# Two-layer graph convolution on one core: last groups of 12 and 7 tiles, an early head of layer 2, layer 2 without node loads, and a first index column

## Chip, core and metric

The kernel runs on one core of a Trainium2 chip. The metric is device time in microseconds of one execution; lower is better. Times of "before" are a median of 10 runs. The engines are PE (matmuls), DVE (vector), ACT (activations and copies), POOL (here: memsets, iotas and the issue of gathers) and SP (issue of plain loads and stores).

## What is computed

Two relational graph convolutions over 12500 nodes of 128 features and 200000 edges sorted by destination, with 10 relations, a residual and a layer norm:

```python
def _rgcn_layer(x, src, dst, edge_type, w_rel, root, bias):
    seg = dst * NUM_REL + edge_type
    sums = segment_sum(x[src], seg)                 # per node and relation
    cnt = segment_sum(ones, seg)
    mean = (sums / maximum(cnt, 1.0)[:, None]).reshape(N, NUM_REL, -1)
    return einsum('nrd,rdo->no', mean, w_rel) + x @ root + bias

edge_type = argmax(msg[:, 16:26], axis=1)
h = relu(_rgcn_layer(x, src, dst, edge_type, w_rel1, root1, b1))
out = layernorm(x + _rgcn_layer(h, src, dst, edge_type, w_rel2, root2, b2))
```

Everything is float32. The mean is over the edges of one node and one relation.

## The kernel before, in words

**Tiles and groups.** 128 edges make a tile; there are NT = 1563 tiles. Tiles go in groups: 95 groups of G = 16 (NS = 95), and then 43 tiles in smaller groups. Before, these are 8, 8, 8, 8, 4, 4 and 3 (L68 to L72). `layer` (L545) runs over the groups once for layer 1 with the table `x`, once for layer 2 with the table `hD`, the hidden nodes in HBM.

**One group.** `gather` (L464) has POOL issue one indirect DMA per tile: 128 rows of the table, chosen by a column of `idxE`, into the buffer `g`, which holds 16 tiles and is taken from a ring of three (`RING = 3`). `ones` (L475) has DVE build, for each tile, `oh`: 128 edges x 120 columns (10 relations x 12 nodes from the tile's first on), with the edge's weight 1/count where it belongs and zero elsewhere (L481), and `at`, which says at which of 160 node columns each of the tile's 12 nodes stands (L485). `sums` (L488) multiplies `g` by `oh` on PE into the PSUM tile `zp` (L495), one matmul per tile, and ACT copies `zp` to `zs` (L509). Groups of 16 wait once for all their gathers; the groups at the end wait for each tile. `project` (L514) multiplies `zs` by the ten relation weights (L521, 20 instructions for up to 8 tiles, 40 for more), ACT copies the result to `ms`, and `add` (L532) multiplies `ms` by `at` (L537) and adds 160 columns to the transposed sums `acc` on DVE (L543). `zp` has one buffer, `oh` two.

**Blocks of nodes.** `starts` cuts the nodes into 29 blocks: 23 of 512, five of 128 and a last of 84. `done_after(k)` says after which tile all edges of block k have been added, with a margin. `block_in` (L394) loads the block's nodes (`xb`; in layer 2 also `hb` from `hD`), transposes them on PE (L407) and copies them to `fT`. `block_rows` adds the bias on DVE (`a`, L416), sets that part of `acc` to zero for layer 2 (L418), and multiplies with the root weights (L421) and the identity (L422). `hidden` (L429) applies ReLU (L435) and stores to `hD`; `final` (L438) adds `xb` (L447), normalises (L450 to L457) and stores. Block 26 is done after the tile 1543, block 28 (the last 84 nodes) after the last tile.

**Set-up.** Edges are prepared in 13 chunks of 128 tiles: `sources` loads the indices as rows, casts them to float, transposes them on PE and casts them back into `idxE` (L165, L172); `types` and `count` find the relation and the count of each edge. Chunk 0 comes ahead of the layers; the others are steps (`todo`), spread over layer 1's groups. ACT fills `acc` with zeros in 25 pieces (L615).

**Order.** Engines run their own queues in order. A scheduler orders the instructions of each engine by program order and by when their inputs are expected, so instructions of one block are interleaved with those of neighbouring groups. Pools decide when a buffer is free: `ps_f` (two PSUM banks, shared by `pf` tiles of blocks and of edge preparation), `gpool` (three), `fin` (one each). SP's queue carries all plain loads and stores in order; a load into a buffer waits for that buffer.

Of the kernel before, what the change touches and what calls it, by code (L numbers as in the profile page):

```python
# [9 lines left out]
F32 = mybir.dt.float32  # L10
BF16 = mybir.dt.bfloat16
I32 = mybir.dt.int32
# [8 lines left out]
P = 128  # L21
# [22 lines left out]
def rgcn_resnorm_kernel(ctx: ExitStack, tc: tile.TileContext, x, src, dst, attr, w_rel1, root1, b1,  # L44
# [25 lines left out]
    while t < NT:  # L70
        groups.append((t, min(HT if NT - t > 3 * QB else QB, NT - t)))
        t += groups[-1][1]  # L72
# [15 lines left out]

    HALF = NT * P - E
    assert C == P and E % GT == 0 and 0 < HALF < P and NT % CT and 1 < groups[-1][1] < groups[-2][1]  # L90

# [26 lines left out]
    wE = keep.tile([P, NCH * CT], F32, name="wE")  # L118

# [54 lines left out]

    ahead = []
# [217 lines left out]

    def block_in(k, l):  # L394

        n0, n, subs = block(k)
        last = "e" if k == NBLK - 1 else ""
        b = len(subs) if last else 4
        xb = fin.tile([P, b, C], F32, name="xb" + last)
        rows_dma(xb, x, k, False)  # L400
        fb = xb
        if l:
            fb = fin.tile([P, b, C], F32, name="hb" + last)
            rows_dma(fb, hD, k, False)
        pt = ps_f.tile([P, YB], F32, name="pf")
        for t, h in subs:
            nc.tensor.transpose(pt[:, t * P:t * P + h], fb[:h, t, :], ident[:h, :h])  # L407
        fT = fin.tile([P, b * P], F32, name="fT" + last)
        nc.scalar.activation(fT[:, :n], pt[:, :n], AF.Copy)  # L409
        return xb, fT  # L410

    def block_rows(fT, k, l):

        n0, n, subs = block(k)
        a = fin.tile([P, YB], F32, name="a")
        nc.vector.tensor_scalar(a[:, :n], acc[:, n0:n0 + n], bsb[l], None, op0=ALU.add)  # L416
        if l == 0:
            nc.vector.memset(acc[:, n0:n0 + n], 0.0)  # L418
        pr = ps_f.tile([P, 4, C], F32, name="pf")
        for t, h in subs:  # L420
            nc.tensor.matmul(pr[:h, t, :], fT[:, t * P:t * P + h], rsb[l], start=True, stop=False)  # L421
            nc.tensor.matmul(pr[:h, t, :], a[:, t * P:t * P + h], ident, start=False, stop=True)  # L422
        return pr
# [5 lines left out]
    def hidden(k, ready):  # L429

        xb, fT = ready
        pr = block_rows(fT, k, 0)
        hb = fin.tile([P, 4, C], F32, name="hb")
        for p, s in spans(k):
            nc.scalar.activation(hb[:p, s], pr[:p, s], AF.Relu)  # L435
        rows_dma(hb, hD, k, True)

    def final(k, ready):  # L438

        xb, fT = ready  # L440
        pr = block_rows(fT, k, 1)
        v = fin.tile([P, 4, C], F32, name="v")
        mv = small.tile([P, 4, 2], F32, name="mv")
        rstd = small.tile([P, 4], F32, name="rstd")
        _, n, subs = block(k)
        for p, s in spans(k):
            nc.vector.tensor_tensor(v[:p, s], pr[:p, s], xb[:p, s], op=ALU.add)  # L447
        for t, h in subs:
            st = small.tile([P, nc.vector.BN_STATS_DIM], F32, name="st")
            nc.vector.bn_stats(st[:h], v[:h, t, :])  # L450
            nc.vector.bn_aggr(mv[:h, t, :], st[:h])
        for p, s in spans(k):
            nc.scalar.activation(rstd[:p, s], mv[:p, s, 1], AF.Sqrt, bias=eps[:p])  # L453
            nc.vector.reciprocal(rstd[:p, s], rstd[:p, s])
        o = fin.tile([P, 4, C], F32, name="o")
        for t, h in subs:
            nc.vector.tensor_scalar(o[:h, t, :], v[:h, t, :], mv[:h, t, 0:1], rstd[:h, t:t + 1],  # L457
                                    op0=ALU.subtract, op1=ALU.mult)
        rows_dma(o, out, k, True)
# [3 lines left out]

    def gather(table, t0, n):  # L464
        g = gpool.tile([P, G, C], F32, name="g")
        return g, [then("POOL", nc.gpsimd.indirect_dma_start(  # L466
            out=g[:, j, :], out_offset=None, in_=table, in_offset=bass.IndirectOffsetOnAxis(
                ap=idxE[:, t0 + j:t0 + j + 1], axis=0))) for j in range(n)]
# [6 lines left out]
    def ones(k):  # L475

        t0, n = groups[k]
        oh = dpool.tile([P, G, KW], F32, name="oh")
        for j in range(n):
            t = t0 + j  # L480
            then("DVE", nc.vector.tensor_scalar(oh[:, j, :], iotaP[:, :KW], keyE[:, t:t + 1], wE[:, t:t + 1],  # L481
                                                op0=ALU.is_equal, op1=ALU.mult))
        at = spool.tile([HR, 2, SW], F32, name="at")
        for h, _ in halves(n):
            nc.vector.tensor_scalar(at[:, h, :], iotaP[:HR], place[:, h, k:k + 1], None, op0=ALU.is_equal)  # L485
        return oh, at

    def sums(table, k, oh, at):  # L488

        t0, n = groups[k]  # L490
        end = k >= NS
        g, gathers = gather(table, t0, n)
        zp = ps_z.tile([P, G // QB, YB], F32, name="zp")
        for j in range(n) if end else reversed(range(n)):
            m = nc.tensor.matmul(zp[:, j // QB, j % QB * KW:(j % QB + 1) * KW], g[:, j, :], oh[:, j, :],  # L495
                                 start=True, stop=True)
            then("PE", m)
            if end:
                continue
            if j < n - 1:  # L500
                tc.keep_in_program_order(m)
                continue

            for d in gathers[:j]:
                tc.add_manual_dep(m.ins, d.ins.name, whole, reason="one wait per group")
        zs = zpool.tile([P, NREL, G, WN], F32, name="zs")
        for b in range(-(-n // QB)):
            m = min(QB, n - b * QB)
            then("ACT", nc.scalar.activation(  # L509
                zs[:, :, b * QB:b * QB + m, :],  # L510
                zp[:, b, :m * KW].rearrange("c (j r n) -> c r j n", r=NREL, n=WN), AF.Copy))
        return k, zs, at
# [32 lines left out]
    def layer(table, l, finish, steps, flag_too=False):  # L545
# [8 lines left out]
        def add_oldest():  # L554
# [3 lines left out]
            while done < NBLK and sum(groups[k]) >= done_after(done):  # L558
                finish(done, ready if done == NBLK - 1 else given or block_in(done, l))
# [3 lines left out]
        for k in range(NG):  # L563
            end = k >= NS
            if k and not given and done < NBLK - 1:
                given = block_in(done, l)
            if projected:
                add_oldest()
            if end:
# [4 lines left out]
                if not ready:  # L574
                    ready = block_in(NBLK - 1, l)
# [6 lines left out]
            held.append(sums(table, k, *(made or ones(k))))  # L582
            made = ones(k + 1) if end and k < NG - 1 else None
# [27 lines left out]
    zero = fin.tile([P, YB], F32, name="a")  # L611
    nc.vector.memset(zero, 0.0)
    for a in range(0, NPAD, YB):
        m = min(NPAD - a, YB)
        nc.scalar.activation(acc[:, a:a + m], zero[:, :m], AF.Copy)  # L615
# [3 lines left out]
    weights_in()  # L619
    todo = []  # L620
    for c in range(1, NCH):
        s = [as_steps(sources, c + 1)] if c + 1 < NCH else []
        todo.append((c * CT // G - 2, [8 + L // DB + 2], chain(*s, types(c), count(c))))
# [22 lines left out]

    gp = ctx.enter_context(tc.tile_pool(name="gp", bufs=2))
# [120 lines left out]
    with tc.If(flag > 0):  # L768
# [3 lines left out]
        for l, (table, finish) in enumerate(((x, hidden), (hD, final))):  # L772
            nc.vector.memset(acc, 0.0)
# [29 lines left out]
```

## Time and profile before

| what | value |
|---|---|
| median of 10 runs | 3946.68 us (3943.41 to 3948.06) |
| the profiled execution | 3947.26 us |
| its span in the profile | 3945.4 us |
| POOL busy | 2957.1 us, 75% |
| PE busy | 2350.4 us, 60% |
| DVE busy | 1513.5 us, 38% |
| ACT busy | 528.5 us, 13% |
| gathers of layer 1 / layer 2 | 1563 / 1563, mean 946 / 944 ns |
| `zp` matmuls (L495) | 6252 instructions, 1149.2 us |
| projection matmuls (L521) | 7880 instructions, 899.0 us |
| `oh` (L481) | 3126, mean 391 ns |

The profile is of one execution; its times are from the start of its span. A line of the page's list of groups gives the source line, engine and operation, output<-input, shape and count, then busy time and mean duration in ns, then the engine's idle time ahead of these and what ended most of it. A line of the timeline gives start, duration, engine, line, operation and, in brackets, the idle time before it and what ended that. "issue" is time in which an engine waited for nothing that the profile shows. A float32 matmul appears as two instructions, a transpose as one.

### The profile page before, as it was taken

How to read it: one execution, taken by the hardware profiler on the slowest of the kernel's cores; microseconds unless marked ns; L12 is line 12 of the kernel's file. 1: busy time of each engine (PE TensorE's matmuls, PEld its weight loads, DVE VectorE, ACT ScalarE, POOL GpSimd, SP SyncE). 2: the span in 40 equal slices, each digit the busy share in tenths (PEclk: the TensorE clock that was granted, in tenths of full speed). 3: DMA queues.
4: the chain of work that ended last, by engine and by line, in shares of the span. 5: the costliest groups of instructions: out<-in, count | busy, mean ns of one | idle time of the engine just before them, and what ended most of it. 6: DMA issues, size and time to landing. Idle time of an engine off the chain costs nothing.

```text
span 3945.4 us, 43799 instructions
## 1 busy us (share of the span) xinstructions
PE 2350.4 (60%) x16206; PEld 2258.4 (57%) x16206; DVE 1513.5 (38%) x4660; ACT 528.5 (13%) x1142; POOL 2957.1 (75%) x3142
## 2 busy tenths in 40 slices
PE   4666665665666666566745565565655565556557
PEld 3655555565566565565635555555555555555556
DVE  6434444343443434443423333333333333333333
ACT  2111111111111111111101111111111111111111
POOL 7777777777777777777677777777777777777775
PEclk8877777777777777777867777777777777777778
DMA  5322323223223232222222222222222222222222
GB/s 163 90 73 75 95 59 89 88 66 90 74 74 95 58 89 64 63 62 57 63 58 58 61 69 61 61 61 64 66 61 61 61 69 61 61 61 69 61 59 55
DMA packets 180538, 278.99 MB, mean 71 GB/s; under 512 B 55608, under 2 KB 127175, under 8 KB 177191
## 3 DMA queue, kind: packets, MB, share of 16 engines
q0 software_dynamic: 100032, 205.07, 19.8%
q1 hardware_dynamic: 78577, 71.03, 5.6%
q8 instruction: 132, 2.16, 0.2%
q14 instruction: 89, 0.73, 0.1%
q10 hardware_dynamic: 1708, 0.01, 0.0%
HBM read 262.28 MB, written 13.60 MB: 70 GB/s over the span
## 4 chain that ended last, share of the span: by engine, by line
POOL 68%; issue 26%; DMA 3%; PE 2%; ACT 0%; DVE 0%; POOLq 0%; ACTq 0%
POOL g L466 68%; DMA g<-hD,idxE 2%; DMA g<-in_x_dram,idxE 1%; PE pp L521 1%; PE zp L495 1%; PE pp L537 0%; ACT zs L509 0%; PE pf L422 0%; PE pf L421 0%; DVE acc L543 0%; POOLq L466 0%; ACT ms L527 0%; DVE o L457 0%; ACT rstd L453 0%; DVE st L450 0%
## 5 line engine op out<-in xcount | busy, mean ns | idle before, releaser
L495 PE MATMUL zp<-oh,g 128*128 128x120 f32 x6252 | 1149.2, 360 | 1517.4 <-DMA g<-hD,idxE 802.4
L495 PEld LDWEIGHTS zp<-oh,g 128*128 128x128 f32 x6252 | 1108.0, 274 | 1556.1 <-issue 1475.7
L466 POOL DMA_INDIRECT g<-hD,idxE x1563 | 1475.7, 944 | 488.4 <-issue 477.3
L466 POOL DMA_INDIRECT g<-in_x_dram,idxE x1563 | 1478.6, 946 | 476.9 <-issue 468.1
L481 DVE TENSOR_SCALAR oh<-bank,keyE,wE 128x120 f32<-128x120 f32 x3126 | 1002.5, 391 | 719.7 <-PE zp L495 719.5
L521 PE MATMUL pp<-w,zs 128*96 128x128 f32 x7880 | 899.0, 273 | 17.5 <-ACT zs L509 14.3
L521 PEld LDWEIGHTS pp<-w,zs 128*96 128x96 f32 x7880 | 871.1, 163 | 23.4 <-ACT zs L509 18.5
L509 ACT ACTIVATE zs<-zp 128x480 f32<-128x480 f32 (+1 forms) x782 | 386.0, 576 | 2508.7 <-PE zp L495 2508.4
L543 DVE TENSOR_TENSOR acc<-acc,pp 128x160 f32 x204 | 65.4, 321 | 1379.2 <-PE pp L537 1378.9
L537 PE MATMUL pp<-at,ms 96*128 96x160 f32 (+1 forms) x788 | 211.0, 407 | 6.9 <-ACT ms L527 5.1
L537 PEld LDWEIGHTS pp<-at,ms 96*128 96x128 f32 (+1 forms) x788 | 171.1, 271 | 22.9 <-ACT ms L527 15.9
L527 ACT ACTIVATE ms<-pp 96x256 f32<-96x256 f32 (+1 forms) x198 | 74.3, 375 | 451.1 <-PE pp L521 451.1
L485 DVE TENSOR_SCALAR at<-bank,place 96x160 f32<-96x160 f32 x394 | 132.7, 369 | 0.0
L362 DVE TENSOR_TENSOR eqb<-pf,kh 128x1344 bf16<-128x1344 f32 (+2 forms) x65 | 100.2, 1549 | 75.4 <-PE pf L366 67.7
L422 PE MATMUL pf<-ident,a 128*128 128x128 f32 x392 | 83.0, 296 | 2.0 <-DVE a L416 1.9
L421 PE MATMUL pf<-root,fT 128*128 128x128 f32 x388 | 80.1, 290 | 1.1 <-ACT fT L409 1.1
L422 PEld LDWEIGHTS pf<-ident,a 128*128 128x128 f32 x392 | 66.2, 212 | 3.5 <-DVE a L416 2.9
L421 PEld LDWEIGHTS pf<-root,fT 128*128 128x128 f32 x388 | 64.3, 208 | 2.0 <-ACT fT L409 2.0
L435 ACT ACTIVATE hb<-pf 128x512 f32<-128x512 f32 (+2 forms) x29 | 15.4, 530 | 340.8 <-PE pf L422 338.6
L364 PE MATMUL pf<-eqb,identb 128*128 128x512 bf16 (+2 forms) x130 | 50.3, 387 | 11.1 <-DVE eqb L362 11.1
L366 PE MATMUL pf<-eqb,identb 128*128 128x512 bf16 (+2 forms) x130 | 50.5, 389 | 0.0
L447 DVE TENSOR_TENSOR v<-pf,xb 128x512 f32<-128x512 f32 (+1 forms) x28 | 17.4, 620 | 73.7 <-PE pf L422 73.6
(107 smaller groups left out, 453.8 us busy)
## 6 DMA issues: line engine op xcount, KB each, us to landing
m<-in_edge_attr_dram SPq DMA_DIRECT2D x24, 1344.0 KB
g<-in_x_dram,idxE POOLq DMA_INDIRECT x1563
g<-hD,idxE POOLq DMA_INDIRECT x1563
xb<-in_x_dram SPq DMA_DIRECT2D x46, 256.0 KB
hD<-hb SPq DMA_DIRECT2D x23, 256.0 KB
hb<-hD SPq DMA_DIRECT2D x23, 256.0 KB
out_dram<-o SPq DMA_DIRECT2D x23, 256.0 KB
w<-in_L_gnn_w_rel_dram SPq DMA_DIRECT2D x2, 640.0 KB
```

What stands on the lines that cost most here:

```text
L362: nc.vector.tensor_tensor(eq[:p], kp[:p, None, :R].to_broadcast([p, DB, R]), fore, op=ALU.is_equal)
L421: nc.tensor.matmul(pr[:h, t, :], fT[:, t * P:t * P + h], rsb[l], start=True, stop=False)
L422: nc.tensor.matmul(pr[:h, t, :], a[:, t * P:t * P + h], ident, start=False, stop=True)
L466: return g, [then("POOL", nc.gpsimd.indirect_dma_start(out=g[:, j, :], out_offset=None, in_=table, in_offset=bass.IndirectOffsetOnAxis(ap= ...
L481: then("DVE", nc.vector.tensor_scalar(oh[:, j, :], iotaP[:, :KW], keyE[:, t:t + 1], wE[:, t:t + 1], op0=ALU.is_equal, op1=ALU.mult))
L485: nc.vector.tensor_scalar(at[:, h, :], iotaP[:HR], place[:, h, k:k + 1], None, op0=ALU.is_equal)
L495: m = nc.tensor.matmul(zp[:, j // QB, j % QB * KW:(j % QB + 1) * KW], g[:, j, :], oh[:, j, :], start=True, stop=True)
L509: then("ACT", nc.scalar.activation(zs[:, :, b * QB:b * QB + m, :], zp[:, b, :m * KW].rearrange("c (j r n) -> c r j n", r=NREL, n=WN), AF.C ...
L521: nc.tensor.matmul(po[:m * WN, h], zs[:, r, h * HT:h * HT + m].rearrange("c j n -> c (j n)"), wsb[l][:, r, :], start=(r == 0), stop=(r == ...
L527: nc.scalar.activation(ms[:, :n // HT], po[:HR, :n // HT], AF.Copy)
L537: nc.tensor.matmul(pa, ms[:m * WN, h], at[:m * WN, h], start=(h == 0), stop=(h == len(parts) - 1))
L543: nc.vector.tensor_tensor(acc[:, s], acc[:, s], pa, op=ALU.add)
```

## The change

1. The last 43 tiles make groups of 8, 8, 8, 12 and 7, five groups instead of seven. Two consecutive groups that fit into 16 tiles share one buffer `g`.
2. The first 16 tiles of layer 2 gather only from the first EARLY = 12288 nodes, with indices held below that (`idxH`) and weights set to zero for edges from later nodes (`wH`). Those edges' part comes from `late_h`, the last two blocks (128 + 84 = 212 nodes) kept in SBUF, by matmuls with `late_w`, tables built by `head()` during layer 1's last full groups.
3. Layer 2 loads no nodes. `hidden` now also transposes its result, multiplies it by layer 2's root weights, and writes that plus layer 2's bias plus the node itself into `acc` in place of the zeros. `final` transposes `acc` by a matmul with the identity and normalises from PSUM. Layer 1's bias is put into `acc` by the fill at the start, which therefore comes after the weights' loads in the program.
4. The indices of the first tile are also loaded directly as a column, `idx0`, and only the first gather of layer 1 uses it.
5. Chunk 12 of the edge preparation is to end four groups earlier, and `head()` is one more step behind it.

The part of the program behind `tc.If(flag > 0)` is a slow path for other inputs; it doesn't run here.

```diff
     while t < NT:
-        groups.append((t, min(HT if NT - t > 3 * QB else QB, NT - t)))
+        n = NT - t
+        groups.append((t, HT if n > 2 * HT + QB else HT + QB if n > HT + QB else n))
         t += groups[-1][1]
...
+    EARLY = starts[NBLK - 2]
...
+    idx0 = keep.tile([P, 1], I32, name="idx0")
+    nc.sync.dma_start(idx0, src[0:P].rearrange("(e o) -> e o", o=1))
     ahead = []
     first_index = sources(0)
...
     def block_in(k, l):
+        if l:
+            return None
...
-        if l:
-            fb = fin.tile([P, b, C], F32, name="hb" + last)
-            rows_dma(fb, hD, k, False)
...
-        a = fin.tile([P, YB], F32, name="a")
-        nc.vector.tensor_scalar(a[:, :n], acc[:, n0:n0 + n], bsb[l], None, op0=ALU.add)
-        if l == 0:
-            nc.vector.memset(acc[:, n0:n0 + n], 0.0)
...
+    def hidden(k, fT):
+        n0, n, subs = block(k)
+        pr = ps_f.tile([P, 4, C], F32, name="pf")
+        for t, h in subs:
+            nc.tensor.matmul(pr[:h, t, :], fT[:, t * P:t * P + h], rsb[0], start=True, stop=False)
+            nc.tensor.matmul(pr[:h, t, :], acc[:, n0 + t * P:n0 + t * P + h], ident, start=False, stop=True)
+        i = k - (NBLK - 2)
+        hb = late_h[:, i:i + 1] if i >= 0 and not anew else fin.tile([P, 4, C], F32, name="hb")
         for p, s in spans(k):
             nc.scalar.activation(hb[:p, s], pr[:p, s], AF.Relu)
         rows_dma(hb, hD, k, True)
+        pt = ps_f.tile([P, YB], F32, name="pf")
+        for t, h in subs:
+            nc.tensor.transpose(pt[:, t * P:t * P + h], hb[:h, t, :], ident[:h, :h])
+        hT = fin.tile([P, YB], F32, name="hT")
+        nc.scalar.activation(hT[:, :n], pt[:, :n], AF.Copy)
+        po = ps_f.tile([P, YB], F32, name="pf")
+        nc.tensor.matmul(po[:, :n], rsb[1], hT[:, :n], start=True, stop=True)
+        nc.vector.scalar_tensor_tensor(acc[:, n0:n0 + n], po[:, :n], bsb[1], fT[:, :n], op0=ALU.add, op1=ALU.add)
...
+    def final(k, _):
+        n0, n, subs = block(k)
+        v = ps_f.tile([P, 4, C], F32, name="pf")
...
-            nc.vector.tensor_tensor(v[:p, s], pr[:p, s], xb[:p, s], op=ALU.add)
+            nc.tensor.matmul(v[:h, t, :], acc[:, n0 + t * P:n0 + t * P + h], ident, start=True, stop=True)
...
+    def head():
+        nc.vector.tensor_scalar(idxH, idxE[:, :G], EARLY - 1, None, op0=ALU.min)
...
+        for b in range(0, G, QB):
+            pm = [ps_f.tile([P, YB], F32, name="pf") for _ in range(2)]
+            for j in range(QB):
+                t = b + j
+                oh = prep.tile([P, KW], F32, name="ohH")
+                nc.vector.tensor_scalar(oh, iotaP[:, :KW], keyE[:, t:t + 1], wE[:, t:t + 1],
+                                        op0=ALU.is_equal, op1=ALU.mult)
+                for i in range(2):
+                    of = prep.tile([P, P], F32, name=f"of{i}")
+                    nc.vector.tensor_scalar(of, iotaP[:, :P], off[:, i, t:t + 1], None, op0=ALU.is_equal)
+                    nc.tensor.matmul(pm[i][:, j * KW:(j + 1) * KW], of, oh, start=True, stop=True)
+            for i in range(2):
+                nc.scalar.activation(late_w[i][:, b * KW:(b + QB) * KW], pm[i][:, :QB * KW], AF.Copy)
+            yield
...
     def gather(table, t0, n):
-        g = gpool.tile([P, G, C], F32, name="g")
+        o = shared.get("to", G)
+        if o + n > G:
+            o = 0
+            shared["g"] = gpool.tile([P, G, C], F32, name="g")
+        shared["to"] = o + n
+        g = shared["g"][:, o:o + n]
+        ix = idxE
+        if is_head(table, t0):
+            table, ix = table[:EARLY, :], idxH
...
+                    nc.tensor.matmul(z[:, :QB * KW], late_h[:n, i, :], late_w[i][:n, b * QB * KW:(b + 1) * QB * KW],
+                                     start=(i == 0), stop=False)
...
-        nc.scalar.activation(acc[:, a:a + m], zero[:, :m], AF.Copy)
     places()
     for _ in chain(types(0), count(0)):
         pass
     weights_in()
+    for a in range(0, NPAD, YB):
+        m = min(NPAD - a, YB)
+        nc.scalar.activation(acc[:, a:a + m], zero[:, :m], AF.Identity, bias=bsb[0])
...
-        todo.append((c * CT // G - 2, [8 + L // DB + 2], chain(*s, types(c), count(c))))
+        todo.append((c * CT // G - (2 if s else 6), [8 + L // DB + 2], chain(*s, types(c), count(c))))
+    todo.append((NS - 1, [G // QB + 1], head()))
```

## Prediction

> **What bounds the kernel now.** I read the page first (span, chain, groups), then the timeline at the four places where the chain leaves its rhythm.
>
> ```profile
> span 3945.4 us, 43799 instructions
> POOL 68%; issue 26%; DMA 3%; PE 2%; ACT 0%; DVE 0%; POOLq 0%; ACTq 0%
> L466 POOL DMA_INDIRECT g<-hD,idxE x1563 | 1475.7, 944 | 488.4 <-issue 477.3
> L466 POOL DMA_INDIRECT g<-in_x_dram,idxE x1563 | 1478.6, 946 | 476.9 <-issue 468.1
> ```
>
> POOL's 3126 gathers of 128 rows are the kernel: 0.944 us each and 0.30 us before the next. In undisturbed stretches of the timeline their starts are 1.248 us apart; 3126 x 1.248 = 3901 us. PE is busy 60%, DVE 38%: neither bounds. The change issues the same 3126 gathers, so only the other 44 us can move: before the first gather, between the layers, after the last one, and stalls in between. The timeline at these places:
>
> ```profile
> 3.78 0.29 DVE L165 CAST idxE<-pf 128x128 int32<-128x128 f32 x1 [0.18 <-PE pf L164]
> 4.36 1.15 POOL L466 DMA_INDIRECT g<-in_x_dram,idxE  x1 [0.92 <-DVE idxE L165]
> ...
> 1945.59 0.28 ACT L435 ACTIVATE hb<-pf 128x128 f32<-128x128 f32 x1 [1.90 <-PE pf L422]
> ...
> 1958.07 0.94 POOL L466 DMA_INDIRECT g<-in_x_dram,idxE  x1 [0.30 <-issue]
> ...
> 1967.20 0.27 ACT L435 ACTIVATE hb<-pf 84x128 f32<-84x128 f32 x1 [1.91 <-PE pf L422]
> ...
> 1969.79 0.94 POOL L466 DMA_INDIRECT g<-hD,idxE  x1 [10.78 <-issue]
> ...
> 3894.24 2.57 DVE L481 TENSOR_SCALAR oh<-bank,keyE,wE 128x120 f32<-128x120 f32 x8
> ...
> 3899.74 0.94 POOL L466 DMA_INDIRECT g<-hD,idxE  x1 [1.95 <-PE zp L495]
> ...
> 3922.20 0.94 POOL L466 DMA_INDIRECT g<-hD,idxE  x1 [0.30 <-issue]
> ...
> 3933.62 2.37 PE L521 MATMUL pp<-w,zs 128*36 128x128 f32 x20 [0.62 <-ACT zs L509]
> ...
> 3939.84 0.39 SPq L392 DMA_DIRECT2D out_dram<-o  x1
> ```
>
> The reader is to see: the first gather waits for a DVE cast; layer 2's first gather starts 11.72 us after layer 1's last, because the last 84 nodes' `hb` is computed at 1967.20 and its store lands only then, while the block before the last two had its `hb` at 1945.59; one gather in the last groups waits for PE to free a buffer; and 23.20 us pass from the last gather's start to the end, since PE is eight microseconds behind.
>
> **The change part by part.**
>
> *First indices as a column.* POOL's last set-up instruction (`lane`) ends at 3.44; the cast ends at 4.07 and the gather starts 0.29 later. The new 512-byte load goes first on SP at 0.83. The load of `s_i`, issued at the same time, let its cast start at 2.64; a 4-byte-element load on ACT's queue (`b_i`, 1520 elements) took until 13.15. With 128 elements I take 3.4, near the first: gather at about 3.75. Bounds -0.9 (POOL free) and +2. `s_i` is issued some 0.45 us later, so the cast ends near 4.5, before the second gather at about 5.2. I take **-0.6 us**.
>
> *Bias in acc, 25 ACT fills.* They take 13 us (11.51 to 24.50) and now wait for `b0` (issued 31.46), behind the copy of `kh` (33.52), and the 1.28 us table load moves behind `kh`'s landing. What is queued behind on ACT: `zs` of group 0, at 57.68. The fills end near 50 to 55. Group 0's matmuls move 1.7 us (0.45 + 1.28). Covered: group 1's matmuls end at 79.1, tile 64 needs that buffer at 84.5, 5.4 us of slack; if `b0` took 20 us longer, each microsecond would be a POOL stall. I take 0, bounds 0 to +3.
>
> *Layer 2's first 16 tiles.* In the compiled order of the changed kernel their first gather waits for the stores up to block 26 and for PE's release of the buffer of tiles 1536-1543; the 17th waits for two further stores. Block 26's store lands near 1948; even with 5 us delay from the longer block chain it is before 1959.3. The 16 gathers take 16 x 1.248 = 20 us, to 1979; the last block's store lands at 1969.8 today, so the 17th has 9 us to spare. The new matmuls (`late_h` x `late_w`, 8 of 128x480, four times an L495 matmul pair of 0.22, so 7 us) lie on PE before 1981, when it idles now (13.79 us idle before 1991). The gap falls from 11.72 to 1.25: **-10.4 us**. Bounds: -10.5, and 0 if a wait covers the late stores.
>
> *head()*: 48 DVE operations of 0.39, 64 matmul instructions of about 0.11, 8 copies of 0.57, over groups 90-94, beside gathers. PE is busy 61% in layer 1, 12 us of each 20 us group; in steady groups PE frees a buffer 32 us before it is needed (group 4's matmuls end at 112.2; tile 112 starts at 144.4). Cost 0.
>
> *hidden longer, final shorter.* Per 512-node block layer 1 gains 4 transposes (0.5 us), a 512-column matmul (0.95), an ACT copy (0.6), loses the 0.50 add and the 0.48 memset; layer 2 loses two loads, 4 transposes, the root matmuls, `a` and `v`. All beside gathers. What remains is their effect on POOL itself:
>
> ```profile
> 1269.47 0.48 DVE L418 MEMSET acc<- 128x512 f32 x1
> 1269.70 1.20 POOL L466 DMA_INDIRECT g<-in_x_dram,idxE  x1 [0.31 <-issue]
> ```
>
> A gather beside a memset takes 1.20 instead of 0.944. Going through all 3126, 34 exceed 0.97 us; 15 of these lie beside `a`, the memset or `o<-v`, and lose 2.2 us together. The Trainium skill, "SBUF — State Buffer", section "SBUF: two separate sides", says that a VectorE operation on SBUF in a two-port mode locks GpSimd out of writing descriptors for its whole duration. By that rule 46 `a` of 0.50, 23 memsets of 0.49 and 97 `o` of 0.28 (four in 1.11) could hold POOL 61 us, and taking `a` and memset away and letting `o` read PSUM would give that back. The rows show 2.2: most such operations fall beside a gather and cost nothing. I take **-2.0** from the rows, bounds -3.5 and +1 (other operations shift against the gathers).
>
> *The end of layer 2.* Groups of 16 fill one buffer in three, and two 8-groups now share one, so tile 1544 waits for group 94 instead of 95: the stall goes, **-1.65 us**. Then the chain on PE, in the frame of the gathers. Group 95's `oh` waits for the final chain of the block before; without 6 matmul instructions, two `a` (0.33) and two `v` (0.33) it comes 2.0 us earlier. From there, `zs` to `zs`: group 95 takes 4.0 (0.9 less, no L407/L421), 96 7.2 (slow clock, as now), 97 5.8, 98 (12 tiles) 7.3; its projection is 40 matmuls, 4.8 after 1.1 of copies, then 3 tiles, two adds (0.9), 3 tiles, the block's transpose, the last tile: 10.0 to `pp` of group 99, about 6 us after the last gather's start. Before it was 3933.62 - 3922.20 = 11.4. After it the end takes 3945.40 - 3933.62 = 11.78 less `a` and `v`, 0.65: 11.1. Here a rule speaks against the change: "VectorE: DVE Perf Modes", section "Why PSUM operands drop a tier": an operand in PSUM caps fp32 at the basic rate. `o` and `st` now read PSUM; `oh<-bank` from PSUM takes 0.32 for 120 columns against 0.28 for `o`. On the path that is one `o`: +0.05. The tail is 17.0 instead of 23.2: **-6.2**. Bounds: -8.8, where the last tile's landing (2.45 after its start) sets the end, and -2.5, where PE stays at the slow clock (20 matmuls in 3.82 as at 3900.59 instead of 2.42).
>
> Sum: -0.6 - 10.4 - 2.0 - 1.65 - 6.2 = -20.9. The profiled execution took 3947.26, 1.86 outside its span; its span becomes 3924.5, its time 3926.4. The median of the runs is 0.58 lower: 3925.8, said as **3926.0**.
>
> **Rivals.**
> *The late stores hold the first gather anyway.* For: waits are per queue lane, and the last stores follow closely. Against: the compiled order names them separately. Then +10.4: 3936.4.
> *The tail only shifts.* For: PE, not POOL, sets it, and a 12-tile group has no neighbour to overlap with. Against: seven groups of fixed cost about 4.8 become five. Then +6.2: about 3932.
> *PE becomes the bound in layer 1* (slower). The longer block chain makes PE wait twice for ACT (`hb`, `hT`), 1.3 us, with 1.5 of matmuls: 2.8 per 512-node block. If it found no idle PE, 22 x 2.8 = 62: 3988. It decides from the point where PE needs over 20 us per group for long enough to use up 32 us of slack; today's 12, plus 0.7, plus 1.8 for head, is 14.5. Against it speaks that no gather of layer 1 waits for PE.
>
> **How the numbers follow.** Forecast 0.74; late stores 0.09; tail only shifts 0.14; PE bound 0.03. The forecast's own ends are 3920 (lock -3.5, tail -8.8) and 3931; the range reaches to the second rival and short of the first: 3920 to 3935. A measurement here can tell 0.2% (8 us) from no change. Faster by that means under 3938.8: all cases but the last and a mishap: 0.94; same 0.03; slower 0.03.
>
> **What would show it.** First gather near 3.75; the two layers' gathers 1.25 us apart; no wait for PE in the last 43 gathers; 17 us from the last gather's start to the end; fewer gathers above 0.97 us. It is wrong if a gather of layer 1 waits for PE, if layer 2's first or 17th gather waits for DMA, or if gathers start at other than 1.248 us.

## The result and the profile after

| | before | after |
|---|---|---|
| median | 3946.96 us (28 runs, 3943.41 to 3950.72) | 3925.1 us (8 runs, 3923.71 to 3926.62) |
| ratio | | 0.9945, 95% interval 0.9936 to 0.9954 |
| span of the profiled execution | 3945.4 us | 3924.9 us |

Forecast 3926.0, measured 3925.1; the span moved by 20.5 us where the sum said 20.9. The profiled execution took 3926.81 us, forecast 3926.4. The page of the changed kernel, the lines that answer to those shown of before:

```profile
span 3924.9 us, 43473 instructions
POOL 68%; issue 26%; PE 3%; DMA 2%; ACT 0%; DVE 0%; POOLq 0%; ACTq 0%
L518 POOL DMA_INDIRECT g<-in_x_dram,idxE x1562 | 1476.0, 945 | 476.0 <-issue 469.3
L518 POOL DMA_INDIRECT g<-hD,idxE x1547 | 1459.7, 944 | 471.4 <-issue 467.8
```

POOL is still the chain, at the same 0.944 us a gather (one gather of layer 1 and 16 of layer 2 have lines of their own now, with `idx0` and `idxH`). The timeline at the places where before left the rhythm:

```profile
3.57 1.15 POOL L518 DMA_INDIRECT g<-in_x_dram,idx  x1 [0.18 <-issue]
...
4.10 0.29 DVE L173 CAST idxE<-pf 128x128 int32<-128x128 f32 x1
...
1943.64 0.28 ACT L441 ACTIVATE hb<-pf 128x128 f32<-128x128 f32 x1 [2.12 <-PE pf L437]
...
1955.80 0.95 POOL L518 DMA_INDIRECT g<-in_x_dram,idxE  x1 [0.30 <-issue]
...
1957.05 0.95 POOL L518 DMA_INDIRECT g<-hD,idxH  x1 [0.30 <-issue]
...
1967.17 0.27 ACT L441 ACTIVATE late_h<-pf 84x128 f32<-84x128 f32 x1 [1.67 <-PE pf L437]
...
3906.89 0.94 POOL L518 DMA_INDIRECT g<-hD,idxE  x1 [0.30 <-issue]
...
3913.81 2.41 PE L585 MATMUL pp<-w,zs 128*84 128x128 f32 x20 [1.26 <-ACT zs L573]
```

The first gather no longer waits for the cast, which now ends after it has started. Layer 2's first gather follows layer 1's last after 1.25 us, ten microseconds before the last nodes' `late_h` exists. From the last gather's start to the end of the span are 18.01 us; before it were 23.20.

| term | predicted | measured | how it is read |
|---|---|---|---|
| first index column | -0.6 | -0.79 | first gather 4.36, then 3.57 |
| between the layers | -10.4 | -10.47 | start to start 11.72, then 1.25 |
| gathers' own times | -2.0 | -2.4 | first to last start of layer 1 1953.71, then 1952.23; of layer 2 1952.41, then 1949.84, less the stall |
| stall before tile 1544 | -1.65 | -1.65 | no gather has more than 0.35 us before it |
| last gather's start to the end | -6.2 | -5.19 | 23.20, then 18.01 |
| sum | -20.9 | -20.5 | spans |

### The profile page after: what moved, and what is told of

It is laid out like the page before. It is cut to its first block, busy times and chain, and to the rows that moved or that the text cites. A ratio compares the mean times of both kernels' runs of the same rounds, so it can differ in the third digit from the quotient of the medians.

```text
span 3924.9 us, 43473 instructions
## 1 busy us (share of the span) xinstructions
PE 2356.6 (60%) x16104; PEld 2251.5 (57%) x16104; DVE 1517.4 (39%) x4621; ACT 536.3 (14%) x1148; POOL 2954.7 (75%) x3142
## 4 chain that ended last, share of the span: by engine, by line
POOL 68%; issue 26%; PE 3%; DMA 2%; ACT 0%; DVE 0%; POOLq 0%; ACTq 0%
POOL g L518 68%; DMA g<-in_x_dram,idxE 1%; PE pp L585 1%; PE zp L558 1%; DMA g<-hD,idxE 1%; PE pp L601 0%; ACT zs L573 0%; PE pf L459 0%; PE pf L502 0%; PE pf L436 0%; DMA g<-hD,idxH 0%; PE pf L449 0%; PE pf L437 0%; PE pf L445 0%; ACT ms L591 0%
## 5 line engine op out<-in xcount | busy, mean ns | idle before, releaser
L558 PE MATMUL zp<-oh,g 128*128 128x120 f32 x6252 | 1128.8, 354 | 1498.1 <-DMA g<-hD,idxE 747.2
L558 PEld LDWEIGHTS zp<-oh,g 128*128 128x128 f32 x6252 | 1084.8, 267 | 1544.6 <-issue 1493.7
L518 POOL DMA_INDIRECT g<-hD,idxE x1547 | 1459.7, 944 | 471.4 <-issue 467.8
L585 PE MATMUL pp<-w,zs 128*96 128x128 f32 x7840 | 904.0, 274 | 17.8 <-ACT zs L573 16.0
L585 PEld LDWEIGHTS pp<-w,zs 128*96 128x96 f32 x7840 | 873.8, 164 | 27.8 <-ACT zs L573 20.1
L601 PE MATMUL pp<-at,ms 96*128 96x160 f32 (+2 forms) x784 | 220.2, 425 | 5.3 <-ACT ms L591 4.6
L601 PEld LDWEIGHTS pp<-at,ms 96*128 96x128 f32 (+2 forms) x784 | 182.0, 289 | 16.0 <-ACT ms L591 9.7
L441 ACT ACTIVATE hb<-pf 128x512 f32<-128x512 f32 (+1 forms) x27 | 14.9, 551 | 320.9 <-PE pf L437 319.2
L437 PE MATMUL pf<-ident,acc 128*128 128x128 f32 x196 | 45.8, 323 | 0.4 <-DVE acc L607 0.4
L450 DVE SCALAR_TENSOR_TENSOR acc<-pf,b,fT 128x512 f32<-128x512 f32 (+1 forms) x28 | 19.0, 679 | 68.9 <-PE pf L449 68.9
L436 PE MATMUL pf<-root,fT 128*128 128x128 f32 x194 | 44.8, 319 | 0.6 <-ACT fT L420 0.6
L462 DVE BATCH_NORM_STATS2 st<-pf 128x6 f32<-128x128 f32 x98 | 24.2, 286 | 48.9 <-PE pf L459 48.9
```

The costliest lines, as they stand in the source:

```text
L518: return g, [then("POOL", nc.gpsimd.indirect_dma_start(out=g[:, j, :], out_offset=None, in_=table, in_offset=bass.IndirectOffsetOnAxis(ap= ...
L585: nc.tensor.matmul(po[:m * WN, h], zs[:, r, h * HT:h * HT + m].rearrange("c j n -> c (j n)"), wsb[l][:, r, :], start=(r == 0), stop=(r == ...
L601: nc.tensor.matmul(pa, ms[:m * WN, h], at[:m * WN, h], start=(h == 0), stop=(h == len(parts) - 1))
```

## The experiments

Each run is compared with before on its own chip. On the chip of the first four, before took 3952.93 us; on the two chips of the other eight it took 4627.4 and 4693, for a reason that the experiments came upon and that is told with them. "Last gather" below means the start of the last gather.

### The gap, by itself: no head

```diff
 def is_head(table, t0):
-    return table is hD and t0 < G
+    return False
...
-    todo.append((NS - 1, [G // QB + 1], head()))
```

> The changed kernel without its head: all tiles of layer 2 gather from all nodes, and neither the late tables nor the eight matmuls with the 212 late nodes are made. If the gap between the layers was the wait for the last nodes' store and nothing is given back later, layer 2's first gather starts 11.7 us after layer 1's last instead of 1.25, the tail stays at 18.0, and the time is 3925.1 + 10.5 = 3935.6. If the head's own work (48 operations on DVE, 72 matmuls) costs something elsewhere, leaving it out gives that back and the time is below 3933.

3942.3 us, ratio 0.9974 (0.9965 to 0.9984). The timeline of this run between the layers:

```profile
1955.41 0.94 POOL L518 DMA_INDIRECT g<-in_x_dram,idxE  x1 [0.30 <-issue]
...
1964.03 0.27 ACT L441 ACTIVATE late_h<-pf 84x128 f32<-84x128 f32 x1 [1.49 <-PE pf L437]
...
1966.57 0.94 POOL L518 DMA_INDIRECT g<-hD,idxE  x1 [10.22 <-DMA hD<-late_h]
```

The releaser is named: the store of the last nodes. The gap is 11.16 us, 9.9 more than with the head; the span is 9.5 longer than the changed kernel's, and the tail 18.04, as there. Almost nothing is given back: without the head, layer 1 takes 1951.84 us from its first to its last gather's start, with it 1952.23. (The ratios differ by 0.0029, 11 us; each is against a before of its own, and the interval of each is some 4 us to either side.)

### The group sizes, by themselves

```diff
-        groups.append((t, HT if n > 2 * HT + QB else HT + QB if n > HT + QB else n))
+        groups.append((t, min(HT if n > 3 * QB else QB, n)))
```

> The changed kernel with the seven old groups at the end (8, 8, 8, 8, 4, 4, 3); buffers are still shared, so the wait of tile 1544 should stay away. By the prediction's sum, 2.0 of the 6.2 us of the tail come from the earlier oh and 0.65 from the shorter last chain, so the group sizes are worth 3.5: 3928.6, with 21.5 us from the last gather's start to the end. If the sizes carry the whole tail: 3930.3 and 23.2. If they carry nothing: 3925 and 18.0.

3934.95 us, ratio 0.9956 (0.9943 to 0.9970); the profiled execution has a span of 3926.5, no stall before tile 1544, and 20.05 us after the last gather. That is 2.0 us more than in the changed kernel, not 3.5. But the two tails aren't alike but for the sizes. The projection of group 95 in this run:

```profile
3883.61 2.42 PE L585 MATMUL pp<-w,zs 128*96 128x128 f32 x20 [1.18 <-ACT zs L573]
```

The same 20 matmuls take 4.57 us in the changed kernel, since PE's clock is lower there at that moment. With that clock this tail would be up to 2.2 us longer, so the sizes are worth between 2.0 and 4.2 us, and the expected 3.5 lies within. The stall goes by the shared buffer and not by the sizes. The clock is the next subject.

### The missing microsecond of the tail: PE's clock

The busy times of the changed kernel in steps of 4 us, from 35 us before the last gather on; the columns are the stretch, its length, busy us (and instructions) of PE, weight loads, DVE, ACT and POOL, the granted clock of PE, DMA share and GB/s:

```profile
3870.00:3874.00 4.00, 4.00 (x39) 4.00 (x39) 1.05 (x4) 0.29 (x1) 3.09 (x4) 1.00 0.25 73
3874.00:3878.00 4.00, 1.86 (x12) 1.21 (x10) 1.04 (x5) 0.67 (x2) 2.97 (x4) 0.99 0.18 49
3878.00:3882.00 4.00, 3.19 (x15) 3.19 (x16) 3.98 (x13) 0.00 (x0) 2.90 (x4) 0.50 0.26 70
3882.00:3886.00 4.00, 2.82 (x13) 2.54 (x13) 2.92 (x10) 1.03 (x2) 3.09 (x4) 0.50 0.19 49
3886.00:3890.00 4.00, 4.00 (x25) 3.83 (x25) 0.67 (x3) 0.27 (x1) 3.08 (x4) 0.73 0.24 60
3890.00:3894.00 4.00, 2.82 (x26) 2.63 (x25) 3.37 (x13) 1.21 (x3) 3.09 (x4) 1.00 0.22 61
```

PE is busy for only 1.86 of 4 us while the chain of a node block passes between PE, DVE and ACT and while it waits for group 95's `oh`; then its clock is half for 10.2 us (3878.0 to 3888.2), and the `zp` and projection matmuls of group 95 are done at that speed:

```profile
3878.35 2.57 DVE L534 TENSOR_SCALAR oh<-bank,keyE,wE 128x120 f32<-128x120 f32 x8
...
3878.81 3.77 PE L558 MATMUL zp<-oh,g 128*128 128x120 f32 x16 [2.00 <-DVE oh L534]
...
3883.76 4.57 PE L585 MATMUL pp<-w,zs 128*96 128x128 f32 x20 [1.18 <-ACT zs L573]
...
3892.03 2.42 PE L585 MATMUL pp<-w,zs 128*96 128x128 f32 x20 [1.18 <-ACT zs L573]
```

The 20 matmuls of one group take 4.57 us, those of the next 2.42. How long the half clock lasts is not fixed by what PE does. The run with the old groups has the same instructions on PE up to here, 0.08 us later, with the same 2.00 us of waiting for `oh`, and the clock fell there too; but it was back at 3882.0, ahead of the projection. The same columns for that run:

```profile
3874.00:3878.00 4.00, 1.94 (x12) 1.29 (x10) 0.97 (x4) 0.67 (x2) 3.08 (x4) 1.00 0.18 49
3878.00:3882.00 4.00, 3.11 (x14) 3.12 (x15) 3.98 (x13) 0.00 (x0) 3.09 (x4) 0.58 0.27 74
3882.00:3886.00 4.00, 2.82 (x26) 2.63 (x25) 3.00 (x10) 1.03 (x2) 3.08 (x4) 0.99 0.20 57
```

The half clock lasted 3.4 us there and 10.2 in the changed kernel. Over that kernel's whole trace the stretches of half clock last 3.41, 6.83, 10.24 or 13.65 us (11, 42, 129 and 6 of them; one more is cut off by the end), all multiples of 3.41. So the clock changes in such steps, and the same wait can cost one of them or three: part of the missing microsecond is chance.

The experiment takes the cause of the wait away: group 95's `oh` is built one group earlier, ahead of the block's chain on DVE.

```diff
-            made = ones(k + 1, table) if end and k < NG - 1 else None
+            made = ones(k + 1, table) if NS - 1 <= k < NG - 1 else None
```

> The changed kernel with the oh of the first 8-tile group at the end built one group earlier, ahead of the node chains on DVE. If the missing microsecond of the tail is PE waiting 2.0 us for that oh and then running 20 matmuls at half clock (4.57 instead of 2.42 us), the groups come 2 to 4.5 us earlier, until the landing of the tiles sets the pace: pp of the last group 4.3 to 5 us after the last gather's start instead of 6.9, 15.4 to 16.1 to the end, 3922.5 to 3923.2. If the clock falls whatever PE waits for, only the 2.0 of the wait are gained at most: 3923.1 to 3925.

3931.53 us, ratio 0.9946 (0.9933 to 0.9960), no different from the change within what can be measured. The tail is 17.1 us, 0.9 shorter. The timeline of this run (its last gather starts at 3912.50):

```profile
3885.97 2.42 PE L585 MATMUL pp<-w,zs 128*96 128x128 f32 x20 [1.18 <-ACT zs L573]
...
3904.41 1.10 PE L558 MATMUL zp<-oh,g 128*128 128x120 f32 x4 [1.12 <-DMA g<-hD,idxE]
...
3906.32 0.48 PE L558 MATMUL zp<-oh,g 128*128 128x120 f32 x2 [0.81 <-DMA g<-hD,idxE]
...
3907.99 6.41 PE L585 MATMUL pp<-w,zs 128*96 128x128 f32 x40 [1.18 <-ACT zs L573]
```

The wait and the half clock at group 95 are gone: its projection comes 26.5 us before the last gather instead of 23.1, and takes 2.42. Seen from the end, those 3.4 us are not kept. PE is now early enough to wait for the tiles of the group of 12 (1.12 and 0.81 us) and then for ACT's `zs` (1.18), and the clock is half from 3908.2 to 3911.6: 40 matmuls in 6.41 us instead of 4.74. `pp` of the last group comes 6.06 us after the last gather, against 6.92 and an expected 4.3 to 5. A stall that was taken away became a wait for data, and the clock took most of the rest.

### Does DVE hold POOL? Memsets and copies

```diff
+        for _ in range(4):
+            nc.vector.memset(zero, 0.0)
         at = spool.tile([HR, 2, SW], F32, name="at")
```

> The changed kernel with four more memsets of 128x512 float32 per group on DVE, 800 in all, into a tile that nothing reads any more. By the rows of before, where 166 such operations cost the gathers 2.2 us together, 800 cost 10.6 us: 3936. [...]

3933.6 us, ratio 0.9953 (0.9939 to 0.9967): 3928.4 where before takes 3946.96, 7.6 us below the 3936 of the row's rate. This execution and that of the early `oh` issue gathers at the same pace (1.2502 us apart), so their streams can be set against each other: from first to last start 1957.94 and 1955.06 us in layer 1, 1952.77 and 1952.62 in layer 2. The 800 memsets, 388 us of DVE time of which 296 lie beside gathers, cost the gathers 3.0 us instead of 10.6. Of the 383 gathers with one of these memsets beside them, three take over 0.03 us longer. The tail was 15.4 us, 2.6 shorter than the change's: the extra work made the order of PE's queue a little different, with the last 512-node block's chain one group earlier. That was seen in the order, and not tested by itself.

The rule of the Trainium skill that the prediction weighed ("SBUF — State Buffer", section "SBUF: two separate sides") is one of two-port modes, and the operations that it names for them include copies from SBUF to SBUF, but not memsets. So copies too:

```diff
+        for _ in range(8):
+            nc.vector.tensor_copy(zero[:, :YB // 2], zero[:, YB // 2:])
         at = spool.tile([HR, 2, SW], F32, name="at")
```

> The changed kernel with eight more float32 copies of 128x256 from SBUF to SBUF on DVE per group, 1600 in all, within a tile that nothing reads any more. 800 memsets of 128x512 before this cost the gathers about 3 us. If copies behave like those, 1600 shorter ones cost 2 to 6 us: 3927 to 3931, ratio 0.995 to 0.996. By the Trainium skill's rule, which names just this copy, POOL is held for its whole duration: 1600 of about 0.28 us, 340 us if only those count that meet a gather at work, 448 if all do: about 4265 to 4375.

Ratio 1.0365 (1.0350 to 1.0379), on a chip where PE set the pace (below), so that the time says little about POOL. The gathers' own durations still do. The two groups of this run:

```profile
L518 POOL DMA_INDIRECT g<-in_x_dram,idxE x1562 | 1496.9, 958 | 959.4 <-issue 445.2 <-PE zp L560 346.7 <-remote 73.0
...
L537 DVE COPY zero<-zero 128x256 f32<-128x256 f32 x1600 | 493.1, 308 | 6.3 <-DVE at L540 2.3 <-remote 2.2 <-DVE oh L534 0.3
```

A gather takes 958 ns on the mean instead of 945. 181 gathers exceed 0.97 us, 178 of them beside one of the copies; their excess over 0.944 is 32.3 us, against 1.2 in a run of the changed kernel itself on another chip of that kind (the last but one below). So 493 us of copies cost 31 us, 6%: more than the 2 to 6 us expected from the memsets, and far less than the 347 us for which copies lie beside gathers in this trace. The rule of the Trainium skill ("SBUF — State Buffer", section "SBUF: two separate sides"), read as in the expectation, would make all of these the loss. The measurement decides: copies delay gathers, and ten times as much as the memsets did, but not for as long as the two lie side by side. Where the cost falls shows in a stretch of the changed kernel:

```profile
178.06 0.95 POOL L518 DMA_INDIRECT g<-in_x_dram,idxE  x1 [0.30 <-issue]
...
179.32 1.59 POOL L518 DMA_INDIRECT g<-in_x_dram,idxE  x1 [0.30 <-issue]
179.39 0.28 DVE L340 TENSOR_TENSOR bad<-d_f 128x128 f32<-128x128 f32 x1
179.59 0.28 DVE L334 SCALAR_TENSOR_TENSOR key<-ty,key 128x128 f32<-128x128 f32 x1
```

DVE operations on SBUF begin 0.07 us after the gather and follow without a pause, and it takes 0.65 us longer. The four other long gathers looked at (at 12.50, 74.06, 861.65 and 1282.72) have such a start 0.09 to 0.11 us behind theirs. The run with the copies lets the place be counted, over its 298 gathers with a single copy beside them. Where the copy began up to 0.15 us ahead of the gather, 19 of 21 take over 0.03 us longer; up to 0.15 us after its start, 20 of 104; 0.15 to 0.45 us after it, none of 35; 0.60 to 0.70 us after it, 7 of 39; later, none of 46. So a gather is open to this at its beginning and, less often, at about 0.65 us. A gather that is caught can lose more than one operation's time: four of that run take 2.70 us, each beside copies and operations of edge preparation that follow one another without a pause for over 2 us. Whether the copies ran in a two-port mode is not shown by the trace.

### Other groups at the end, and a chip where PE sets the pace

```diff
-        n = NT - t
-        groups.append((t, HT if n > 2 * HT + QB else HT + QB if n > HT + QB else n))
+        n = [12, 12, 8, 8, 3][len(groups) - NS]
+        groups.append((t, n))
```

These two runs also have the early `oh`; the third is one part of the change alone.

> The kernel with the early oh (the run before this), with the last groups 12, 12, 8, 8 and 3 instead of 8, 8, 8, 12 and 7. In that run the group of 12 waited for its tiles and then multiplied at half clock, and pp of the last group came 6.06 us after the last gather. If the landing of the tiles sets the pace now, a short group before the last and 3 tiles in the last bring pp of the last group 4.2 to 4.8 us after the last gather, and the end 15.3 to 15.9 after it instead of 17.1; against before 0.9942. If PE's own work sets it (two groups of 12 early, each some 7.3 us), pp comes 6 us or more after the last gather and the end at 17 or later.

> As the run with 12, 12, 8, 8 and 3, but with 8, 8, 12, 8 and 7: the last group's seven tiles leave PE waiting for some 3 us before the last tile lands. If the landing alone counts, pp of the last group comes 4.2 to 4.8 us after the last gather; if that wait also lowers PE's clock, its 20 matmuls take 4.6 us instead of 2.4 and the end comes 17.5 to 18 us after the last gather in spite of it.

> Only one part of the change: layer 2 loads no nodes. The groups at the end are the seven old ones with a buffer each, the first 16 tiles of layer 2 gather from all nodes, and the first gather takes its indices from the transposed rows. If the parts add up as in the prediction, this part is worth 2.0 to 2.4 us in the gathers' own times, and 2.0 + 0.65 of the tail, together 4.7 to 5: ratio 0.9988, with the gap of 11.2 to 11.7 us between the layers, the stall of 1.65 us before tile 1544 and a tail of 20 to 20.5 us. If the longer work per block in layer 1 costs something that the other parts hide, a gather of layer 1 waits and the time is at or above that of before.

Ratios 1.0295 (1.0281 to 1.0310), 1.0293 (1.0279 to 1.0307) and 1.0215 (1.0199 to 1.0231), to a before of 4627.4 us. Only the last possibility named for the third came true: gathers wait, and the time is above that of before. The other expectations are neither met nor refuted, since here gathers wait for PE throughout. Two of the runs were made again, and a third chip behaved like this one:

> The groups of 12, 12, 8, 8 and 3 with the early oh once more, since on the chip of the runs before this, PE got an instruction of the projection only every 0.70 us while gathers ran and set the pace. Where before takes about 3950 and no gather waits for PE: pp of the last group 4.2 to 4.8 us after the last gather and the end at 15.3 to 15.9, ratio 0.9940 to 0.9945, if the landing sets the pace; 6 us and 17, ratio 0.9945, if PE's own work does. Where PE is slow again: ratio 1.029.

> Only the part by which layer 2 loads no nodes, once more for the same reason. Where before takes about 3950: ratio 0.9988 (-4.7 to -5 us: gathers 2.0 to 2.4, tail 2.65), the gap of 11.2 to 11.7 us and the stall before tile 1544 still there, no gather of layer 1 waiting for PE. At or above 1.000 if the longer work per block costs something there. Where PE is slow again: ratio 1.021.

1.0206 (1.0189 to 1.0224) and 1.0134 (1.0115 to 1.0153), to a before of 4693.39: slower again, but less than the 1.029 and 1.021 expected for that case. What those end groups are worth where POOL sets the pace stays unmeasured. The last two runs ask what costs the time here:

> The changed kernel itself, once more, beside a run in which one part is undone. Where before takes about 3950 us and no gather waits for PE: ratio 0.9945. Where PE gets instructions of the projection only every 0.70 us and sets the pace: layer 2 without node loads alone gave 1.013 and 1.022 there, the version with new groups and early oh 1.021 and 1.030; so 1.02 to 1.03, since the head and the groups can win nothing on POOL while POOL waits.

4792.62 us, ratio 1.0216 (1.0201 to 1.0231), to a before of 4693.7, as expected for a slow PE. On this chip the change makes the kernel slower. For the second, `block_in`, `block_rows`, `hidden` and `final` of before were put back, and the fill of `acc` with zeros:

```diff
-        if l:
-            return None
+        fb = xb
+        if l:
+            fb = fin.tile([P, b, C], F32, name="hb" + last)
+            rows_dma(fb, hD, k, False)
...
-        nc.scalar.activation(acc[:, a:a + m], zero[:, :m], AF.Identity, bias=bsb[0])
+        nc.scalar.activation(acc[:, a:a + m], zero[:, :m], AF.Copy)
```

> The changed kernel with one part undone: layer 2 loads its nodes again, hidden and final are those of before (bias, zeros and node added where they were); the new groups, the head and the first index column stay. Where no gather waits for PE: the gathers lose 2.0 to 2.4 us and the tail 2.65, so 4.7 to 5 more than the changed kernel, ratio 0.9957. Where PE sets the pace: if the longer work per block in layer 1 is what costs there, it is gone and the ratio falls to 1.000 to 1.008, the rest being the head's 72 matmuls; if it stays at 1.02 the cost lies in the head or in the end groups.

4727.74 us, ratio 1.0080 (1.0065 to 1.0096), at the edge of what was expected. Of the 99 us, 65 go with the part that was undone. The streams of the three runs on this chip:

| run | layer 1, first to last start | gap | layer 2 | last gather to end |
|---|---|---|---|---|
| the change | 2449.5 | 13.2 | 2286.8 | 33.4 |
| with node loads | 2372.8 | 13.5 | 2307.0 | 32.5 |
| nodes only | 2417.5 | 20.1 | 2292.4 | 24.2 |

The longer `hidden` costs layer 1 76.6 us and the shorter `final` returns 20.2 in layer 2. (The gathers of these executions differ in pace, 1.2507 us with the change and 1.2481 with node loads, which is an estimated 4 us for each layer at most.) PE's waits in the run of the change show where: it waits for ACT's `hb` ahead of the new transposes.

```profile
PE pf L445 <- ACT hb L441: 87.5, 14, 12.4
```

(us in total, times, longest.) The run with node loads has no such transposes, and in the result's profile that wait doesn't show. The change over "nodes only" adds 31.9 in layer 1: 23 of it by tile 1541, up to which the head's 64 matmuls are done, and 9 behind that, among the new end groups. No run takes the two apart.

Why PE is the bound there: a stretch of the change's run on that chip, PE's rows and the first of ACT and POOL after them.

```profile
2597.22 5.61 PE L558 MATMUL zp<-oh,g 128*128 128x120 f32 x28
2602.66 0.93 PE L585 MATMUL pp<-w,zs 128*96 128x128 f32 x7
2604.05 0.27 PE L585 MATMUL pp<-w,zs 128*96 128x128 f32 x1 [0.46 <-issue]
2605.45 0.38 PE L585 MATMUL pp<-w,zs 128*96 128x128 f32 x2 [1.14 <-issue]
2606.87 0.27 PE L585 MATMUL pp<-w,zs 128*96 128x128 f32 x1 [1.04 <-issue]
2608.28 0.45 PE L585 MATMUL pp<-w,zs 128*96 128x128 f32 x2 [1.14 <-issue]
2610.41 0.37 PE L585 MATMUL pp<-w,zs 128*96 128x128 f32 x1 [1.67 <-issue]
2611.12 1.08 PE L585 MATMUL pp<-w,zs 128*96 128x128 f32 x3 [0.34 <-issue]
2612.53 4.23 PE L585 MATMUL pp<-w,zs 128*96 128x128 f32 x23 [0.33 <-issue]
...
2612.73 1.96 ACT L573 ACTIVATE zs<-zp 128x480 f32<-128x480 f32 x4 [16.79 <-remote]
...
2612.90 0.95 POOL L518 DMA_INDIRECT g<-hD,idxE  x1 [3.43 <-remote]
```

The first 17 of a group's 40 projection matmuls take 9.9 us, with starts some multiple of 0.70 us apart and nothing that the profile shows to wait for; the other 23 take 4.23. ACT copies `zp` at 2612.73, though its last matmul ended at 2602.83; in the result's profile the copy follows 0.1 us behind (3.57 us of matmuls from 2600.31, `zs` at 2603.98). POOL starts again at the same moment. So, as far as the matmuls' ends in the profile, which are modelled, can be trusted, it isn't only that PE gets on slowly: what it has finished becomes known to the others 10 us late, and all at once. A group takes 23.1 us there, and 20 us is the point that the prediction named for the third rival. Over the run, in the same columns:

```profile
PE pp L585 <- issue: 817.6, 834, 5.8
...
POOL g L518 <- remote: 497.4, 143, 8.2
...
POOL g L518 <- PE zp L558: 299.8, 39, 18.9
```

In the result's profile the projection's whole idle time is 17.8 us. The transfers that bring instructions are no slower there: 131 packets of a mean 1.01 us, in the result's profile 131 of 1.09. No profile of before was taken on those chips. What holds PE there isn't shown by these traces and stays open.

## Why the prediction was right

*The bound.* 3126 gathers 1.248 us apart, and only the other 44 us can move: so it was on the chips where before takes about 3950.

*First index column.* -0.79 for -0.6. The load landed in time for POOL to go on 0.18 us after its last set-up instruction, and the cast for the second gather ended at 4.39, 0.63 ahead of it. It lies inside the bounds; no run undid it alone.

*ACT fills and head().* Both costed at nothing, and no gather in the result's profile has more than 0.35 us before it. The last of `late_h` comes 11.37 us after layer 1's last gather, 2.75 later than in the run without the head; that the head's matmuls are in its way on PE is likely and not shown. The delay is hidden too: the seventeenth gather of layer 2 comes 21 us after that last one.

*The gap.* -10.47 for -10.4. The run without the head shows the named store as the releaser, and 9.9 us come back.

*DVE's effect on the gathers.* -2.4 for -2.0. 15 gathers exceed 0.97 us where before 34 did, and what they exceed 0.944 by falls from 4.8 us to 2.4. The run with node loads takes this part by itself: 27 such gathers with 3.4 us, against 11 to 15 with 1.1 to 1.9 in the three other runs on its chip, which load none. Weighing row against rule was the choice that mattered, 2 us against 61, and the copies bear it out in size: 6% of their time was lost. But two readings behind it were wrong. The 61 us count 23 memsets, 11 us of them, which the rule doesn't name. And the gather of 1.20 us was put down to the memset in the row above it, while DVE also began an operation of edge preparation (L315 of the kernel before) 0.17 us after the gather's start. By the run with 800 memsets, a memset alone does next to nothing; what the two do together was not tested.

*The stall.* -1.65 as said; it stays away with the old sizes, so it was the sharing.

*The tail.* -5.19 for -6.2, the one term that was mis-sized. The chain was right: `oh` of group 95 comes 2.2 us earlier in the frame of the gathers (2.0 said), `zs` of that group 4.3 after it (4.0), then 5.9, 7.0 and 10.0 us for groups 97, 98 and 99 (5.8, 7.3, 10.0), and 11.1 from there; the last `o`, which now reads PSUM, takes 0.41 us where it took 0.34, for a predicted +0.05. What failed is "96 7.2 (slow clock, as now)", which took 8.27: in the result the half clock lasts through all of group 95's projection, 4.57 us where before it took 3.82. The sum carried the clock over from before as a number, and after the same wait the clock can be half for 3.4 or 10.2 us. The same is why the run with the old sizes, where it was back before group 95's projection, can't say more of the sizes than 2.0 to 4.2.

*The sum.* It fits better than its terms: the tail's +1.0 us is set off by -0.4 of the gathers, -0.2 of the first index and -0.1 of the gap. That they cancel is luck.

*The rivals.* The late stores didn't hold the first gather. The tail did more than shift, but by a microsecond less than forecast. PE as the bound did not come about on the chip of the prediction and did on two others. Its price was 62 us in layer 1, 22 times 2.8; undoing the longer `hidden` and the shorter `final` gave 76.6 there (65 in the time of the kernel, since layer 2 then takes 20.2 longer). The kind of wait was right, PE for ACT's `hb`, but not its size: 14 waits of 6.3 us on the mean where 1.3 us for each block was said. And PE is over the point of 20 us per group not by the longer block chain, as the rival had it, but by whatever holds it on those chips. That the sums lie near each other is no support for the rival's reasoning.

## What to carry to other kernels

Find the stretches where the bounding engine leaves its rhythm, name what ends each, and add up only those: here five such terms gave 20.9 us, and 20.5 were measured, though the terms' errors partly cancelled. Work moved to an engine "that idles anyway" is free only as long as its slack holds; say from what time per group it stops being free, because another chip may be past that point. A matmul's duration near the end of a program is no constant: PE's idle microseconds ahead of it can be paid twice, once as waiting and once as a lower clock, and the second price differs from run to run.

## What the runs showed of the hardware

- The pace of the gathers differs between executions of one chip: 1.2483 us from start to start in the profiles of before, of the change and of the first two experiments, 1.2502 in the next two. Over 3126 gathers that is 6 us, more than most of the terms here; where POOL sets the pace, streams may be compared only at the same one.
- PE's granted clock was 0.5 after a few microseconds with little work, and stayed there for 3.41, 6.83, 10.24 or 13.65 us in the changed kernel's trace. In a steady group it was back at 1.0 3.9 us after the work set in (work from 2617.93, a mean of 0.77 from 2620 to 2624, so back at about 2621.8); at the end, where the work had gaps, after 9.4 us (3878.8 to 3888.2), and in the run with the old groups after 3.1 (3878.9 to 3882.0).
- A DVE copy cost a gather time mainly where it began within 0.15 us of the gather's start (39 of 125 with a single copy beside them, 9 of 173 elsewhere); of 69 with a single memset in the same place none took over 0.03 us longer. 800 memsets of 128x512 cost 3126 gathers 3.0 us, 1600 copies of 128x256 31.
- On two of the chips PE's matmuls started at multiples of 0.70 us for up to 10 us at a time, its results became known late, and the kernel before took 17 to 19% longer than on the others.
